# Four conditional transformer blocks on one core: queries and keys sent in two halves, and the filling work paced to the last step

## The chip, the cores and the metric

The kernel runs on one NeuronCore of a Trainium2 chip. The metric is the device time of one execution in microseconds. TensorE (PE) multiplies and transposes, VectorE (DVE) and ScalarE (ACT) work on its results in PSUM, GpSimd (POOL) adds, and SyncE (SP) issues nearly all DMAs from one queue, in order.

## The reference

The input `x` is 4 sequences of 512 tokens with 288 features, with one condition vector of 288 for each sequence. Four layers follow each other, all in float32.

```python
x = L0(x, cond)   # a conditional rotation: x + (z @ expm(A(cond)) - z) @ U.T, z = x @ U, U from a QR
x = L1(x, cond)   # attention with 16 heads of 18, then an MLP of 1152, both modulated and gated
x = L2(x, cond)   # the same, with a layer norm on each head's queries and keys
x = L3(x, cond)   # attention, then a mixture of 4 experts, 2 for each token
# in each attention:
qkv = modulate(layernorm(x)) @ w_qkv + b_qkv
attn = softmax(q @ k.T * 18 ** -0.5)
x = x + gate * ((attn @ v) @ w_proj + b_proj)
```

In the code the attention layers are counted 0, 1, 2 (reference layers 1, 2, 3). Layer 1 of the code is the one that normalizes queries and keys: each projected block needs the variance over the 18 features of a head.

## The kernel before

After the rotation the kernel goes through 12 items, n = 0 to 11: item n is sequence n % 4 in layer n // 4. `attend(n, ...)` does the attention of item n in 32 steps, 8 for each of 4 groups (G) of 4 heads. In every step PE computes one pair of score tiles `p_s` for the group that comes 10 steps later (`maxima`); DVE reduces the pair to its row maxima (`TENSOR_REDUCE store<-p_s`). In the same step PE computes one pair of transposed scores `p_st` (`weigh`), and ACT takes its exponential into `e`. In even steps `give_values` multiplies the weights of two earlier steps with the values (`p_av`). In step 6 of each group, steps 6, 14, 22 and 30 of an item, `take_maxima` transposes the maxima of the next group (`p_m`) and DVE subtracts them. `p_s` and `p_st` share two PSUM pairs, so `p_s` of a step needs the reduction of the step before to be over. A step is here the stretch from one `p_st` to the next.

Since the maxima run 10 steps ahead, step 22 of item n already reads queries and keys of item n + 1. All else is filling work, drawn from generators that yield a cost in microseconds. `attend` adds `total / 32` to a balance `left` in every step, and half a microsecond more in odd steps and less in even ones, and draws from `fill` until the balance is spent. The fill of item n is, in this order: the first part of `project(n + 1)`, up to where it yields `None`; `finish(n - 1)`, which multiplies the attention output of the item before with `w_proj` (`p_o`, four times) and adds it to `x`; the rest of `project(n + 1)`; and `layernorm(n - 1)`, the transposes `p_t` that feed the MLP. Small DVE steps (`normalize`, which makes `xn`, and `invert`, which multiplies `oc` by `rb`) come from a second list, one in each step. After the 32 steps, what is left of the fill is drawn at once, and `mlp(n - 1)` follows. After item 11 come the experts.

`project(n)` computes five blocks of queries and keys, `p_qk` 0 to 4 (126 rows each, the last 72), and four blocks of values, `p_v`. Each is two matmuls over 128 features (called `qk` and `v` below) and a tail over the last 32; the blocks go in pairs, so that the two tails run beside each other. A block is evicted into a `stage` tile and written to a DRAM scratch `qd` (L1076), from where eight DMAs bring the heads to their rows of `Q` and `K` (L1113) and four more clear a row (L1115). Queries are rows 0 to 287 of `qd`, keys 288 to 575. In layer 1 the eviction has three parts: ACT squares and DVE adds the bias; then PE sums the squares (`p_var`) and ACT makes the factor; then DVE scales (`SCALAR_TENSOR_TENSOR stage`) and POOL adds (L1075). The second part is drawn while the next pair is multiplied. In every item the third pair (`p_qk` 4, `p_v` 0) is finished at once, and then all is sent. Blocks `p_qk`, `p_v`, `p_var`, `p_o`, `p_m`, `p_t` share three PSUM banks (`pmm`).

The order of DMAs on SP's queue is made by the framework's scheduler, not by the text. The order on PE and DVE inside an attend follows the text.

Of the kernel before, what the change touches and what calls it, by code (L numbers as in the profile page):

```python
# [9 lines left out]
F32 = mybir.dt.float32  # L10
# [6 lines left out]
B, T, C = 4, 512, 288  # L17
# [4 lines left out]
H, HD, HS = 16, 18, 32  # L22
VS = HD + 1
NG = 4
HP = 7
QP = HP * HD
QK = 2 * C
NQ = -(-QK // QP)
# [19 lines left out]
def cond_seq_kernel(ctx: ExitStack, tc: tile.TileContext, a: dict, out: bass.AP):  # L48
# [18 lines left out]
    dma = nc.sync.dma_start  # L67
# [11 lines left out]
    def pmm(name):  # L79
        return ps.tile([128, 512], F32, tag="mm", name=name, bufs=3)  # L80
# [4 lines left out]
    def pacc(name):  # L85
        return ps.tile([128, 512], F32, tag="acc", name=name, bufs=1)
# [49 lines left out]
    def strip(i):  # L136
        return slice(i * TAIL, (i + 1) * TAIL)
# [89 lines left out]
    Q = [t[:, 0:NG * T].rearrange("p (g t) -> p g t", t=T) for t in store]  # L227
    K = [t[:, NG * T:2 * NG * T].rearrange("p (g t) -> p g t", t=T) for t in store]
# [7 lines left out]
    zero_row = rows.tile([4, NG * T], F32, name="zero_row")  # L236
# [432 lines left out]
    def layernorm(l, part, b, dst, norm):  # L669

        for _ in norm:
            pass
        for _ in to_featT(dst, b, XN.pop((l, part, b)), modT[l][:, 2 * part + 1], modT[l][:, 2 * part], 2 + part):
            yield 0.6
# [353 lines left out]
    with tc.tile_pool(name="attn", bufs=2) as at:  # L1028
# [15 lines left out]
        def project(n, norm):  # L1044

            l, b = divmod(n, B)
            wqk, wv = WA[l][:2]
            h = hT[0]
            yield from layernorm(l, 0, b, h, norm)
            qd = scratch.tile([2 * H, HD, T], F32, tag="qd", name=f"qd{n}")  # L1050
            flat = qd.rearrange("h d t -> (h d) t")

            def qk_job(m):
                w = min(QP, QK - m * QP)
                cols = slice(m * QP, m * QP + w)
                p = pmm(f"p_qk{n}_{m}")

                def evict():
                    bias = QB[l][0:w, m:m + 1]
                    t = at.tile([QP, T], F32, tag="stage", name=f"stage{n}_{m}", bufs=3)[0:w]  # L1060
                    if l != 1:
                        scalar.activation(t, p[0:w], AF.Identity, bias=bias, scale=scol[0:w, m:m + 1])
                    else:
                        tmp = at.tile([128, 2, T], F32, tag="e", name=f"tmp{n}_{m}", bufs=6)
                        sq, rs = tmp[0:w, 0, :], tmp[0:w, 1, :]
                        scalar.activation(sq, p[0:w], AF.Square, bias=bias)
                        vector.tensor_scalar(t, p[0:w], bias, None, ALU.add)
                        yield 0.0
                        pv = pmm(f"p_var{n}_{m}")
                        matmul(pv[0:w], varsel.rearrange("p h d -> p (h d)")[0:w, 0:w], sq, start=True, stop=True)  # L1070
                        scalar.activation(rs, pv[0:w], AF.Ln, bias=eps5[0:w])
                        scalar.activation(rs, rs, AF.Exp, scale=-0.5)
                        yield 0.86
                        vector.scalar_tensor_tensor(t, t, gains[0][0:w, m:m + 1], rs, ALU.mult, ALU.mult)
                        nc.gpsimd.tensor_scalar(t, t, gains[1][0:w, m:m + 1], None, ALU.add)  # L1075
                    dma(flat[cols], t)  # L1076
                return p[0:w], 0.86, lambda k, r: (wqk[r, k, cols], h[r, k, :]), evict

            def v_job(j):
                p = pmm(f"p_v{n}_{j}")  # L1080

                def evict():
                    (scalar.copy if j % 2 else vector.tensor_copy)(
                        V[n % 2][:, j, :, 0:HD], p[:, :C].rearrange("p (h d) -> p h d", d=HD))
                    yield from ()
                return p[:, :C], 0.49, lambda k, r: (h[r, k, j * 128:(j + 1) * 128], wv[r, k, :]), evict

            jobs = [(qk_job, m) for m in range(NQ)] + [(v_job, j) for j in range(NT)]
            later = []
            for i in range(0, len(jobs), 2):  # L1090
                pair = []
                for job, arg in jobs[i:i + 2]:
                    p, cost, operands, evict = job(arg)
                    for k in range(KW):
                        matmul(p, *operands(k, slice(0, 128)), start=(k == 0), stop=False)
                        yield cost
                    pair.append((p, operands, evict))
                for e in later:
                    yield from e
                for q, (p, operands, evict) in enumerate(pair):  # L1100
                    matmul(p, *operands(KW, strip(q)), start=False, stop=True)

                later = [e for e in [evict() for p, operands, evict in pair] if next(e, None) is not None]
                yield 0.95
                if i <= NQ - 1 < i + 2:
                    for e in later:
                        yield from e
                    later = []

                    src = qd.rearrange("(s g i) d t -> s i d g t", s=2, i=4)  # L1110
                    for s, t in enumerate((Q[n % 2], K[n % 2])):
                        for q in range(4):
                            dma(t[q * HS:q * HS + HD], src[s, q])  # L1113
                    for q in range(4):
                        dma(Q[n % 2][q * HS + HD:q * HS + VS], zero_row[q:q + 1].rearrange("a (g t) -> a g t", t=T))  # L1115
                    there.add(n)
                    yield None

        def maxima(G, step):

# [8 lines left out]
        def take_maxima(G):  # L1129

            n, g = divmod(G, NG)
            p = pmm(f"p_m{G}")
            for j in range(NT):
                transpose(p[:, j * 128:(j + 1) * 128], M[G % 2][:, j].rearrange("p h r -> p (h r)"), ident)
            vector.tensor_sub(Q[n % 2][:, g, :], Q[n % 2][:, g, :], p)
# [71 lines left out]
        def attend(n, fill, total, norms):  # L1207

            left = 0.0
            for step in range(8 * NG):  # L1210
                g, s = divmod(step, 8)
                G = NG * n + g
                ahead, mstep = divmod(8 * G + s + LOOK, 8)
                if ahead < NG * NB:
                    while ahead // NG not in there:
                        next(fill)
                    maxima(ahead, mstep)
                E.append(weigh(G, s))
                if s == 8 - 2 and G + 1 < NG * NB:
                    take_maxima(G + 1)  # L1220
                if s % 2 == 0:
                    give_values()
                left += total / (8 * NG) + (0.5 if s % 2 else -0.5)
                next(norms, None)
                while left > 0:
                    cost = next(fill, "end")
                    if cost == "end":
                        break
                    left -= cost or 0.0
                if s % 2:  # L1230
                    ready.append((G, s // 2))
            for _ in fill:
                pass
            for _ in norms:
                pass

        def give_values():

            if not ready:
                return  # L1240
            G, c = ready.pop()
            if c == 0:
                PO[0] = pacc(f"p_av{G}")
            sum_values(G, PO[0], c, E[:2])
            del E[:2]
            if c == NT - 1:
                t = at.tile([128, T], F32, tag="o", name=f"o{G}", bufs=3)
                scalar.copy(t, PO[0])
                n, g = divmod(G, NG)
                if g == 0:  # L1250
                    S[n] = (scratch.tile([H, T], F32, tag="sd", name=f"sd{n}"),
                            scratch.tile([H, HD, T], F32, tag="od", name=f"od{n}"))
                dma(S[n][0][4 * g:4 * g + 4, :], t.rearrange("(h r) c -> h r c", r=HS)[:, HD])
                for h in range(4):
                    dma(S[n][1][4 * g + h], t[h * HS:h * HS + HD])
# [29 lines left out]
        E, ready, PO, S, there, norms = [], [], [None], {}, set(), {}  # L1285
# [33 lines left out]
        for n in range(NB):  # L1319
            l, b = divmod(n, B)  # L1320
# [48 lines left out]
            if 2 <= n < 2 + 2 * NE:  # L1369
                fill_table(n - 2)  # L1370
            attend(n, itertools.chain(*fill), total, first_ready(side))
            if n == 2 or n == B + 2:
                projection_bias(l + 1)
# [183 lines left out]
```

## Time and profile before

| | us |
|---|---|
| median of 3 runs (2065.1 to 2071.37) | 2068.3 |
| the profiled execution, its own time | 2073.4 |
| its span, first to last instruction | 2071.7 |
| attends 1, 2, 7, 8, step 0 to step 31 | 91.2, 87.3, 87.2, 87.2 |
| attends 3, 4, 5, 6 (they project layer 1) | 92.9, 93.3, 103.7, 93.0 |
| attends 9, 10, 11 | 87.4, 97.8, 101.0 |

The page gives busy times over the whole span. What an attend does is read from the timeline, step by step: a step that is longer than its matmuls has idle time on PE, and the bracket behind the next `p_s` says how long and what ended it. The windows view gives the mean granted clock of PE for a stretch.

### The profile page before, as it was taken

What the parts mean: (1) busy time and instruction counts of PE and PEld (TensorE: products, weight loads), DVE (VectorE), ACT (ScalarE), POOL (GpSimd) and SP (SyncE); (2) the same over time, 40 slices, a digit from 0 to 9 for tenths busy, and PEclk for the clock granted to TensorE, in tenths of its full rate; (3) what the DMA queues carried; (4) which work ended last, traced back from release to release, by engine and by line L of the source; (5) the groups of instructions that cost most, each with busy time, mean ns of one, the idle gap of its engine ahead of it and who ended that gap; (6) DMA issues with size and microseconds to landing.
All of it is one profiled execution on the core that took longest, in us unless ns stands there. A gap on an engine that the chain in (4) does not pass through costs nothing. (4 is left out here: it accounts for less than half of the span.)

```text
span 2071.7 us, 26248 instructions
## 1 busy us (share of the span) xinstructions
PE 1887.7 (91%) x10269; PEld 935.6 (45%) x10269; DVE 928.4 (45%) x1953; ACT 783.6 (38%) x1169; POOL 251.9 (12%) x362
## 2 busy tenths in 40 slices
PE   6769879999999999899999999998987888999998
PEld 4544223343523434234234353333332266788886
DVE  6764646346164362552644626345576234211111
ACT  5122454444254343453544434434444222221221
POOL 1000010001010020010100000000000122233232
PEclk9578999999999999999999999999999689999999
DMA  3212152031131221511213112161212265576673
GB/s 97 71 40 62 36 147 84 22 89 36 25 85 30 70 62 42 136 42 54 72 26 77 42 54 81 21 134 35 83 46 66 86 222 167 182 242 200 211 241 97
DMA packets 89419, 187.23 MB, mean 90 GB/s; under 512 B 25453, under 2 KB 50456, under 8 KB 86802
## 3 DMA queue, kind: packets, MB, share of 16 engines
q1 hardware_dynamic: 77462, 103.39, 19.1%
q0 software_dynamic: 11248, 79.79, 11.9%
q10 hardware_dynamic: 584, 2.36, 0.3%
q8 instruction: 81, 1.33, 0.3%
q14 instruction: 44, 0.36, 0.1%
HBM read 152.49 MB, written 55.45 MB: 100 GB/s over the span
## 5 line engine op out<-in xcount | busy, mean ns | idle before, releaser
L60 ACT ACTIVATE e<-p_st 128x1024 f32<-128x1024 f32 x384 | 392.7, 1023 | 650.7 <-PE p_st L60 646.3
L60 DVE TENSOR_REDUCE store<-p_s 128x2 f32<-128x1024 f32 x384 | 470.3, 1225 | 364.5 <-PE p_st L60 320.7
L60 PE MATMUL p_s<-store 32*128 32x512 f32 x1536 | 442.2, 648 | 82.5 <-DVE store L60 81.3
L60 PE MATMUL p_st<-store 32*128 32x512 f32 x1536 | 445.7, 659 | 0.9 <-DVE store L60 0.9
L60 PEld LDWEIGHTS p_s<-store 32*128 32x128 f32 x1536 | 120.0, 185 | 315.3 <-DVE store L60 228.2
L60 PE MATMUL p_av<-e,store 128*32 128x512 f32 x1536 | 212.8, 627 | 2.2 <-ACT e L60 2.2
L60 PE MATMUL p_he<-hTe,store 128*128 128x256 f32 (+1 forms) x1026 | 188.4, 390 | 4.2 <-DVE hTe L60 4.2
L60 PE MATMUL p_ye<-store,hide 128*128 128x288 f32 x684 | 171.4, 409 | 0.0
L60 PEld LDWEIGHTS p_he<-hTe,store 128*128 128x128 f32 (+1 forms) x1026 | 151.4, 191 | 37.7 <-issue 13.6
L695 POOL TENSOR_TENSOR x<-x,gated 128x288 f32<-128x288 f32 x80 | 63.9, 799 | 841.6 <-DVE gated L60 841.6
L60 PE MATMUL p_qk<-hT,wqk 128*126 128x512 f32 (+1 forms) x360 | 163.1, 622 | 0.3 <-DVE store L60 0.3
L60 ACT ACTIVATE hide<-p_he,store 128x256 f32<-128x256 f32 x171 | 68.5, 478 | 245.1 <-PE p_he L60 244.3
L60 PE MATMUL p_h<-hT,w 128*128 128x512 f32 (+1 forms) x432 | 153.5, 610 | 5.2 <-DVE store L60 5.2
L60 PEld LDWEIGHTS p_ye<-store,hide 128*128 128x128 f32 x684 | 128.2, 190 | 36.7 <-ACT hide L60 2.3
L60 PE MATMUL p_y<-w,hid 128*128 128x288 f32 x576 | 141.8, 407 | 0.0
L60 DVE TENSOR_TENSOR gated<-p_y,gate 128x288 f32<-128x288 f32 x32 | 14.6, 457 | 283.0 <-PE p_y L60 283.0
L60 PEld LDWEIGHTS p_y<-w,hid 128*128 128x128 f32 x576 | 108.8, 190 | 35.5 <-issue 6.1
L60 PEld LDWEIGHTS p_st<-store 32*128 32x128 f32 x1536 | 118.2, 187 | 12.1 <-issue 9.1
L60 PEld LDWEIGHTS p_h<-hT,w 128*128 128x128 f32 (+1 forms) x432 | 62.1, 189 | 95.1 <-issue 84.9
L60 PE MATMUL p_o<-wp,oc 126*128 126x288 f32 (+1 forms) x288 | 99.4, 468 | 1.3 <-DVE oc L60 1.3
L60 PEld LDWEIGHTS p_qk<-hT,wqk 128*126 128x126 f32 (+1 forms) x360 | 47.1, 178 | 95.9 <-issue 94.3
L60 DVE COPY hTe<-p_te 128x512 f32<-128x512 f32 x19 | 13.1, 690 | 169.2 <-PE p_tf L60 117.8
(248 smaller groups left out, 1728.8 us busy)
## 6 DMA issues: line engine op xcount, KB each, us to landing
store<-qd SPq DMA_DIRECT2D x96, 144.0 KB
qd<-stage SPq DMA_DIRECT2D x48, 252.0 KB
od<-o SPq DMA_DIRECT2D x192, 36.0 KB
rd<-rd SPq DMA_DIRECT2D x12, 576.0 KB
oc<-od SPq DMA_DIRECT2D x24, 252.0 KB
rb<-rd SPq DMA_DIRECT2D x24, 252.0 KB
etab<-in_L_cond_w_dram SPq DMA_DIRECT2D x4, 1296.0 KB
etab<-in_L_cond_w_dram SPq DMA_DIRECT2D x8, 576.0 KB
```

Of the source, the lines that this page charges most:

```text
L60: ins = f(*args, **kw)
L695: nc.gpsimd.tensor_add(x[b][:, j, :], x[b][:, j, :], t)
```

## The change

The eight DMAs from `qd` become sixteen, in two halves of four each for queries and for keys: half 0 brings head groups 0 and 1, half 1 groups 2 and 3. Half 0 needs blocks 0 to 3 and is sent behind the second pair, half 1 behind the third. In layer 1 the third pair is no longer finished at once: its variance comes behind the main matmuls of the fourth pair, and each half is sent one pair later than in the other layers, half 1 and the `None` in the middle of the fourth pair (`p_v` 1 and 2). There are four `stage` buffers instead of three, and two `o` buffers instead of three. In steps 6, 14 and 22 of an item, and in 30 (where a next group exists), 0.6 is taken off the balance of the fill.

```diff
-                    t = at.tile([QP, T], F32, tag="stage", name=f"stage{n}_{m}", bufs=3)[0:w]
+                    t = at.tile([QP, T], F32, tag="stage", name=f"stage{n}_{m}", bufs=4)[0:w]
...
+            def send(half):
+
+                src = qd.rearrange("(s g i) d t -> s i d g t", s=2, i=4)
+                gs = slice(half * NG // 2, (half + 1) * NG // 2)
+                for s, t in enumerate((Q[n % 2], K[n % 2])):
+                    for q in range(4):
+                        dma(t[q * HS:q * HS + HD, gs], src[s, q, :, gs])
+                for q in range(0 if half else 4):
+                    dma(Q[n % 2][q * HS + HD:q * HS + VS], zero_row[q:q + 1].rearrange("a (g t) -> a g t", t=T))
+                there.add(n)
+
+
+            parts = {(-(-(C + C // 2) // QP) - 1) // 2 * 2: 0, (NQ - 1) // 2 * 2: 1}
...
                 for e in later:
                     yield from e
+                if l == 1 and i - 2 in parts:
+                    send(parts[i - 2])
+                    if parts[i - 2]:
+                        yield None
                 for q, (p, operands, evict) in enumerate(pair):
                     matmul(p, *operands(KW, strip(q)), start=False, stop=True)
 
                 later = [e for e in [evict() for p, operands, evict in pair] if next(e, None) is not None]
                 yield 0.95
-                if i <= NQ - 1 < i + 2:
-                    for e in later:
-                        yield from e
-                    later = []
-
-                    src = qd.rearrange("(s g i) d t -> s i d g t", s=2, i=4)
-                    for s, t in enumerate((Q[n % 2], K[n % 2])):
-                        for q in range(4):
-                            dma(t[q * HS:q * HS + HD], src[s, q])
-                    for q in range(4):
-                        dma(Q[n % 2][q * HS + HD:q * HS + VS], zero_row[q:q + 1].rearrange("a (g t) -> a g t", t=T))
-                    there.add(n)
-                    yield None
+                if l != 1 and i in parts:
+                    send(parts[i])
+                    if parts[i]:
+                        yield None
...
                 if s == 8 - 2 and G + 1 < NG * NB:
                     take_maxima(G + 1)
+                    left -= 0.6
...
-                t = at.tile([128, T], F32, tag="o", name=f"o{G}", bufs=3)
+                t = at.tile([128, T], F32, tag="o", name=f"o{G}", bufs=2)
```

The order of PE's instructions in the two built programs shows how the fill moves. Steps that are not listed keep theirs. Attends 1, 7, 8 are as 2, attends 4 to 6 as 3. In the table `qk` and `v` are one matmul of a block, `tail` the one over the last 32 features, `var` a `p_var`, `o0` to `o3` the four `p_o`, `t0` to `t2` groups of four transposes, `m` the `p_m`. Every even step has `p_av` besides. Lengths are those of the trace before, in us.

| step | attend 2 before | us | after | attend 3 before | us | after | attend 9 before | us | after |
|---|---|---|---|---|---|---|---|---|---|
| 6 | m | 3.4 | m | m | 2.7 | m | m, 2 tails | 3.6 | m |
| 7 | 2 qk | 3.0 | qk | 2 qk | 3.0 | qk | qk | 2.6 | 2 tails, qk |
| 8 | | 2.5 | qk | qk | 3.1 | qk | qk | 3.1 | |
| 9 | 2 qk | 3.0 | qk | var0, var1 | 4.0 | qk, var0 | qk | 2.5 | 2 qk |
| 10 | | 2.5 | qk | | 2.5 | | qk | 3.1 | |
| 11 | 2 tails, qk | 2.9 | 2 tails | 2 tails, qk | 2.9 | var1, 2 tails | 2 tails | 2.5 | qk, 2 tails |
| 12 | | 2.5 | qk | qk | 3.2 | qk | qk | 3.1 | |
| 13 | qk, v | 2.6 | qk | 2 v | 2.5 | qk, v | qk | 2.5 | qk |
| 14 | m, v | 3.3 | m | m, var2 | 4.1 | m | m, v | 3.3 | m |
| 15 | 2 tails, o0 | 3.8 | 2 v, 2 tails | var3, 2 tails | 2.5 | v, var2 | v, 2 tails | 2.5 | qk, v |
| 16 | | 2.5 | | | 4.1 | var3 | | 2.6 | v |
| 17 | o1 | 2.9 | o0 | var4, o0 | 3.7 | 2 tails, v | o0 | 2.9 | 2 tails |
| 18 | | 2.5 | | | 2.5 | v | o1 | 3.9 | o0 |
| 19 | o2 | 2.9 | o1 | o1 | 2.9 | 2 v, var4 | | 2.5 | o1 |
| 20 | o3 | 3.9 | o2 | o2 | 3.9 | | o2 | 3.9 | |
| 21 | | 2.6 | o3 | o3 | 2.9 | o0, o1 | o3 | 2.9 | o2 |
| 22 | m, v | 3.3 | m | m | 2.7 | m | m | 2.7 | m |
| 23 | 3 v | 2.7 | | 2 v | 2.5 | o2 | v | 2.5 | o3 |
| 24 | 2 tails | 2.6 | v | v | 2.7 | | v | 2.7 | |
| 25 | 2 v | 2.3 | 3 v | v, 2 tails, v | 3.1 | o3 | 2 v, 2 tails | 2.5 | v |
| 26 | tail | 2.5 | 2 tails | v | 2.8 | | | 2.7 | v |
| 27 | t0, t1 | 3.5 | 2 v | tail, t0 | 3.4 | 2 tails, v | 2 v | 2.5 | 2 v, 2 tails |
| 28 | | 2.5 | tail | t1 | 2.7 | v | tail | 2.5 | |
| 29 | t2 | 2.5 | t0, t1 | t2 | 2.5 | tail, t0 | | 2.4 | 2 v |
| 30 | m | 3.1 | m | m | 3.1 | m | m | 2.7 | m |
| 31 | MLP | | t2, MLP | MLP | | t1, t2, MLP | | 2.5 | tail |

On DVE the last `xn` of attend 2 stands in step 27 before and in step 28 after. In attend 3 all four stand in step 29 after (one each in steps 25 and 26 and two in 27 before). In attends 0, 10 and 11 the fill moves by one to two steps in the same way.

## The prediction

> **What bounds the kernel now.** I read the page first, then the timeline inside the attends, then their windows.
>
> ```profile
> span 2071.7 us, 26248 instructions
> PE 1887.7 (91%) x10269; PEld 935.6 (45%) x10269; DVE 928.4 (45%) x1953; ACT 783.6 (38%) x1169; POOL 251.9 (12%) x362
> ...
> L60 DVE TENSOR_REDUCE store<-p_s 128x2 f32<-128x1024 f32 x384 | 470.3, 1225 | 364.5 <-PE p_st L60 320.7
> L60 PE MATMUL p_s<-store 32*128 32x512 f32 x1536 | 442.2, 648 | 82.5 <-DVE store L60 81.3
> ```
>
> TensorE (PE) is busy in 91% of the span; of its 184 us of idle, 82.5 stand ahead of `p_s`, nearly all ended by VectorE (DVE) work. The loop is on the timeline of attend 2:
>
> ```profile
> 484.08 0.70 PE L60 MATMUL p_s<-store 32*128 32x512 f32 x2 [0.32 <-DVE store L60]
> ...
> 485.15 1.92 PE L60 MATMUL p_o<-wp,oc 126*128 126x288 f32 x6
> 485.26 1.23 DVE L60 TENSOR_REDUCE store<-p_s 128x2 f32<-128x1024 f32 x1 [0.65 <-PE p_st L60]
> 487.00 0.70 PE L60 MATMUL p_s<-store 32*128 32x512 f32 x2
> ...
> 490.92 0.70 PE L60 MATMUL p_s<-store 32*128 32x512 f32 x2
> ...
> 492.09 1.23 DVE L60 TENSOR_REDUCE store<-p_s 128x2 f32<-128x1024 f32 x1 [0.61 <-PE p_st L60]
> 493.37 0.77 PE L60 MATMUL p_s<-store 32*128 32x512 f32 x2 [1.32 <-DVE store L60]
> ```
>
> A step without filling work lasts 490.92 to 493.37, 2.45 us: `p_s` runs 1.17, its reduction 1.23, and only then is the PSUM pair free. That is the floor. PE itself needs 1.07 for `p_s` and `p_st` (484.08 to 485.15), and in even steps 1.07 more for `p_av`. So an odd step hides about 1.4 us of fill, an even one 0.3; fill beyond that lengthens the step, room left empty is lost. The step with `p_o` (484.08 to 487.00) lasts 2.9.
>
> In the attends that project layer 1 the DVE queue sets some steps:
>
> ```profile
> 612.18 0.75 DVE L60 SCALAR_TENSOR_TENSOR stage<-stage,qn_g,tmp 126x512 f32<-126x512 f32 x1 [0.58 <-ACT tmp L60]
> ...
> 612.85 0.74 DVE L60 TENSOR_SCALAR stage<-p_qk,qkb 72x512 f32<-72x512 f32 x1
> 613.51 0.44 DVE L60 COPY store<-p_v 128x288 f32<-128x288 f32 x1
> 613.87 1.21 DVE L60 TENSOR_REDUCE store<-p_s 128x2 f32<-128x1024 f32 x1
> 615.14 0.19 PEld L60 LDWEIGHTS p_s<-store 32*128 32x128 f32 x2 [2.46 <-DVE store L60]
> ```
>
> Evictions stand ahead of the reduction, and PE waits. Two attends are longer for another reason, by their windows (length, busy time of PE, PEld, DVE, ACT, POOL, then granted clock):
>
> ```profile
> 431.10:518.40 87.30, 80.76 (x489) 28.43 (x490) 53.92 (x78) 44.56 (x54) 6.00 (x11) 1.00 0.27 74
> 563.50:656.40 92.90, 86.57 (x499) 29.37 (x500) 60.39 (x88) 50.40 (x64) 11.73 (x10) 1.00 0.32 66
> 828.70:932.50 103.80, 94.20 (x501) 31.49 (x502) 60.76 (x88) 50.46 (x64) 11.71 (x10) 0.92 0.36 89
> ...
> 1612.00:1650.00 38.00, 36.82 (x100) 11.87 (x104) 5.83 (x19) 9.12 (x12) 6.27 (x7) 0.55 0.31 114
> ```
>
> Attend 5 holds the same work as attend 3 and takes 10.9 us more, at a clock of 0.92; the end of attend 11 ran at 0.55.
>
> **The change, part by part.** I go by the table of steps above: each new step gets the length of a measured step with the same content, or else 1.07 plus its fill.
>
> *Pacing, attends 1, 2, 7, 8.* The 0.6 taken off in steps 6, 14, 22, 30 moves fill later. Steps 7 to 12: two `qk` in one odd step (3.0) and an empty even step (2.5) become one each (2.5 and 3.1 from attend 3's step 8), so 16.4 becomes 16.8; a small loss, since an even step has no room. Steps 13 to 16: 2.6, 3.3, 3.8, 2.5 become 2.5, 2.7, 2.95, 2.5, since `o0` leaves step 15: 12.2 to 10.65. Steps 17 to 22: 2.9, 2.5, 2.9, 3.9, 2.6, 3.3 become 2.9, 2.5, 2.9, 3.9, 2.9, 2.7; step 21 had 1.3 of idle and now holds `o3`: 18.1 to 17.8. Steps 23 to 28: 2.7, 2.6, 2.3, 2.5, 3.5, 2.5 become 2.5, 2.7, 2.7, 2.6, 2.4, 2.5: 16.1 to 15.4. There step 27 waited 1.1 for the last `xn`, issued in that very step; after, `xn` ends in step 28 and the transposes come in 29, which stays at 2.6 (it was 2.5) and holds two transposes instead of one. Step 30 stays at 3.1. Sum 68.4 to 66.35. `t2` (0.6) goes into step 31 ahead of the MLP, where PE waits 0.9 for a reduction now (attends 1, 7, 8): covered there, 0.6 in attend 2. Gain 2.1 each, 8.4 in four.
>
> *Attends 9 and 10.* In attend 9 the even steps 8, 10, 12 held a `qk` and lasted 3.1; emptied, they last 2.5, and the odd steps 7, 9, 11 that take these go from 2.6, 2.5, 2.5 to 3.0. With the rest of its columns steps 6 to 31 go from 73.2 to 70.9: 2.3. Steps 14 to 31 of attend 10 go from 53.5 to some 51; there many small DVE operations of the routing move too, so I take 2.0. Attends 0 and 11 keep their work and their empty steps: 0.
>
> *Layer 1, attends 3, 4, 6.* For: step 9 (4.0, two variances, the second waiting 0.8 for ScalarE) becomes 3.2; step 14 loses `var2` (4.1 to 2.7); step 16 loses its 1.5 of idle but takes `var3` (4.1 to 3.2); step 17 loses `var4` and `o0` (3.7 to 2.5). Against: step 11 now queues `oc` and four stage operations on DVE, 0.66 apart, behind its reduction (2.4) and ahead of the next, which so ends at 2.4 + 3.3 + 1.25 = 6.95; step 11 lasts 2.85 and step 12 the other 4.1, not 3.2. In step 21 two `p_o` meet, and the pair `v1`, `v2` holds two of the three PSUM banks until step 27, so the second, 1.9 long, starts only behind the first one's `gated` at about 3.6: 2.9 to 5.5. In step 29 the first transpose drains the normalization: reduction to 2.4, four `xn` of 0.36 each, the last transpose 0.3: 2.5 to 4.2. Steps 7 to 30 sum to 73.3 before and 72.7 after, and 0.4 of `t1`, `t2` sticks out ahead of the MLP. Gain 0.2 each, 0.6 in three; the bounds are -2 (the three new waits half as long again) and +3 (none of them).
>
> *Fourth buffer, attend 5.* The only wait for a stage buffer that I find is there:
>
> ```profile
> 868.91 0.75 DVE L60 TENSOR_SCALAR stage<-p_qk,qkb 126x512 f32<-126x512 f32 x1 [1.17 <-POOL stage L1075]
> ...
> 870.85 0.29 PEld L60 LDWEIGHTS p_s<-store 32*128 32x128 f32 x2 [4.62 <-DVE store L60]
> ```
>
> The buffer takes the 1.17 away, but the `oc` before it still waits for `rb` until 865.73, and one more stage operation (0.66) stands in the queue: 0.5. I leave the half clock of attend 5 where it is.
>
> *Sending in halves.* 8 more DMAs per projection, about 0.35 us of SP each (four `store<-qd` issue in 1.65), 2.8 per attend on a queue that waits most of the time. Queued behind a send's wait for `qd` are the `o` stores of the group and later `oc<-od`. In attend 2 the last send was issued at 479.1, the DMA share is zero from 485, and the first reader is at 493.37; in attend 3 it is 624.6, 629 and 631.1. In layer 1 the second half now ends about 10 us after step 21 begins, but its first reader is the third head group, 16 steps after step 22. Cost 0; if this cover were gone, up to 5 us in each of the four. Two `o` buffers instead of three: a buffer returns after 16 steps, over 40 us, while its five DMAs issue within 10 us of the copy, even in attend 5: 0.
>
> Sum: 8.4 + 2.3 + 2.0 + 0.6 + 0.5, about 14 us. The profiled execution took 2073.4 us, 1.7 around its span and 5.1 above the median; 2073.4 - 14 is 2059.4, and from the median 2068.3 it is 2054.
>
> **Rivals.** *The steps only trade (same).* The floor stays and no work is removed; if the new steps queue on DVE as attend 3 does now, the four plain attends give 0.5 each, layer 1 loses 2 each, the rest 2: some 4 lost, 4 won, 2062 to 2070. For: steps 7 to 12 lose by my own table. Against: the idle of steps 21 and 27 is plainly in the trace. That the fourth buffer has nothing to remove outside attend 5 belongs here.
>
> *The clock is granted again (much faster).* Attend 5 lost 10.9 us, and from 1612.06 to 1646.82 seven `p_st`, four `p_av`, four `p_o` and one `p_m` took 34.8 us, where their full-speed spacings (1.05, 1.0, 1.84, 0.6) make 19.3. If moved steps miss one or both, 10 to 26 us more: 2028 to 2044. For: attend 4 has a longer idle (1.9) in step 16 than attend 5 (1.6) and stayed at 1.00. Against: what precedes both stretches, the late `rb` and the sparse steps of attend 11, is unchanged, and the three times lie within 0.3%. [...]
>
> *Layer 1 falls to half clock (slower).* After the change attends 3, 4, 6 have new idles: 1.0 in step 12, 1.5 in step 29. Attend 5 shows the price, 10.9 each. It decides from two of three: 2054 + 22 is 2076, with all 2087. For: the second low stretch of attend 5 began after an idle of 1.6. Against: idles of 1.5 to 1.9 in attends 3, 4, 6 did not do it, and neither did 1.1 to 1.3 in the others.
>
> **How the numbers follow.** Forecast (gain 7 to 20) 0.58, clock granted 0.15, trade 0.18, half clock 0.09. A measurement of this kernel tells about 0.3%, 6.2 us, from no change. So faster 0.73, same 0.18, slower 0.09. The range reaches into one clock stretch won (2035) and to the trade (2068).
>
> **What would show it.** Right: attends 1, 2, 7, 8 near 85 us, step 21 filled, no wait for `xn` ahead of the transposes; attends 3, 4, 6 within 2 us of before, step 21 near 5.5, step 29 near 4.2; no `p_s` ended by a DMA. Wrong: plain attends unchanged, `p_s` waiting for `store<-qd`, DVE waiting for POOL's `stage`, or a clock below 1.00 in other attends than 5, 10 and 11.

## The result, and the profile after

| | before | after |
|---|---|---|
| median of 20 runs each, us | 2067.2 (2060.0 to 2081.1) | 2060.0 (2040.7 to 2063.2) |
| the profiled execution, us | 2073.4 | 2047.1 |
| its span, us | 2071.7 | 2045.4 |
| attends 1, 2, 7, 8, step 0 to 31 | 91.2, 87.3, 87.2, 87.2 | 87.7, 84.5, 84.5, 84.5 |
| attends 3, 4, 5, 6 | 92.9, 93.3, 103.7, 93.0 | 91.8, 90.2, 99.5, 90.2 |
| attends 9, 10, 11 | 87.4, 97.8, 101.0 | 84.5, 100.0, 86.6 |

The changed kernel is faster: the ratio is 0.9933, interval 0.9911 to 0.9955, which is 13.9 us of 2067.2. The difference of the medians, 7.2, is smaller because the changed kernel's twenty times lie in two bands, 8 at 2040.7 to 2047.1 and 12 at 2058.6 to 2063.2, and nothing between; the ratio goes over all of them. Their mean granted clocks part as well, 0.956 to 0.959 and 0.945 to 0.948. What parts the bands is the subject of the last experiments. The profiled execution is of the lower one.

From the page of the changed kernel, first its span and busy times, then the two groups of the step:

```profile
span 2045.4 us, 26383 instructions
PE 1876.4 (92%) x10269; PEld 933.1 (46%) x10269; DVE 929.2 (45%) x1953; ACT 784.1 (38%) x1169; POOL 255.5 (12%) x362
...
L60 DVE TENSOR_REDUCE store<-p_s 128x2 f32<-128x1024 f32 x384 | 470.4, 1225 | 360.4 <-PE p_st L60 324.5
L60 PE MATMUL p_s<-store 32*128 32x512 f32 x1536 | 445.5, 653 | 75.5 <-DVE store L60 74.4
```

The work is the same, 10269 matmuls; the idle ahead of `p_s` went from 82.5 to 75.5. On the timeline of attend 2 step 21 begins with the `p_s` at 489.37 and ends with the next:

```profile
489.37 0.70 PE L60 MATMUL p_s<-store 32*128 32x512 f32 x2
...
490.44 1.92 PE L60 MATMUL p_o<-wp,oc 126*128 126x288 f32 x6
492.28 0.70 PE L60 MATMUL p_s<-store 32*128 32x512 f32 x2
```

It now holds `o3` and no idle stands ahead of the next `p_s`; before, this step waited 1.32. In layer 1 the three places that the prediction named are on the timeline of attend 4: DVE's queue of step 11, the second `p_o` of step 21, the first transposes of step 29.

```profile
725.87 0.68 DVE L60 TENSOR_TENSOR oc<-oc,rb 126x512 f32<-126x512 f32 x1
726.47 1.45 DVE L60 SCALAR_TENSOR_TENSOR stage<-stage,qn_g,tmp 126x512 f32<-126x512 f32 x2
727.84 1.40 DVE L60 TENSOR_SCALAR stage<-p_qk,qkb 126x512 f32<-126x512 f32 x2
729.16 1.21 DVE L60 TENSOR_REDUCE store<-p_s 128x2 f32<-128x1024 f32 x1
...
755.82 1.92 PE L60 MATMUL p_o<-wp,oc 126*128 126x288 f32 x6 [0.55 <-DVE gated L60]
...
779.06 1.35 PE L60 MATMUL p_t<-ident,xn 128*128 128x128 f32 x4 [1.17 <-DVE xn L60]
```

The five operations ahead of the reduction (`oc`, two scalings, two additions of the bias) run without a gap, and none waits for a stage buffer. In attend 5 the buffer wait is gone too, but its place is taken by a longer wait for `rb` (DVE, then PE, then SP's queue of DMAs):

```profile
861.57 0.69 DVE L60 TENSOR_TENSOR oc<-oc,rb 126x512 f32<-126x512 f32 x1 [5.46 <-DMA rb<-rd]
...
866.09 1.22 PE L60 MATMUL p_s<-store 32*128 32x512 f32 x2 [6.27 <-DVE store L60]
...
842.57 0.81 SPq L1176 DMA_DIRECT2D rd<-sums  x1
854.58 0.55 SPq L1178 DMA_DIRECT2D rd<-rd  x1
...
858.41 1.18 SPq L1181 DMA_DIRECT2D rb<-rd  x3
```

The windows of attends 2, 4 and 5 and of the end of attend 11 (length, busy times, granted clock, DMA share, GB/s):

```profile
430.80:515.40 84.60, 79.71 (x487) 27.66 (x486) 53.87 (x78) 42.41 (x51) 6.08 (x11) 1.00 0.27 76
...
692.80:783.00 90.20, 84.93 (x490) 28.54 (x489) 59.98 (x88) 47.17 (x60) 12.47 (x11) 1.00 0.25 72
822.90:922.40 99.50, 88.71 (x489) 29.54 (x488) 60.37 (x88) 47.28 (x60) 12.10 (x10) 0.95 0.38 92
...
1582.00:1620.00 38.00, 34.27 (x208) 11.30 (x204) 17.72 (x50) 16.33 (x18) 6.29 (x7) 0.97 0.33 119
```

The last line stands against 0.55 before: in this execution the long half clock at the end of attend 11 is absent.

From start to start the 26.3 us of the two profiled executions divide so: 16.3 are won by the start of attend 11, 14.4 in attend 11 (the clock), and 4.4 are lost among the experts. From the last step to the end the profiled executions below take 420 to 426 us with the same expert code (427.3 and 430.6 in the two where a long half clock runs on into this part), in no order that follows their edits (425.4 here and 420.3 in a kernel below that differs only in layer 1), so I put the 4.4 down to this execution; no run shows its cause. That the 14.4 are the clock's is borne out further down: with extra matmuls that keep the long half clock away, attend 11 takes 84.4 in the kernel before and 84.3 in the changed one.

### The profile page after: what moved, and what is told of

Same layout as the page of the kernel before. It is cut to its first block, busy times and chain, and to the rows that moved or that the text cites. A ratio compares the mean times of both kernels' runs of the same rounds, so it can differ in the third digit from the quotient of the medians.

```text
span 2045.4 us, 26383 instructions
## 1 busy us (share of the span) xinstructions
PE 1876.4 (92%) x10269; PEld 933.1 (46%) x10269; DVE 929.2 (45%) x1953; ACT 784.1 (38%) x1169; POOL 255.5 (12%) x362
## 5 line engine op out<-in xcount | busy, mean ns | idle before, releaser
L60 PE MATMUL p_s<-store 32*128 32x512 f32 x1536 | 445.5, 653 | 75.5 <-DVE store L60 74.4
L60 PE MATMUL p_qk<-hT,wqk 128*126 128x512 f32 (+1 forms) x360 | 167.6, 630 | 0.3 <-DVE store L60 0.3
L60 PE MATMUL p_o<-wp,oc 126*128 126x288 f32 (+1 forms) x288 | 92.6, 442 | 3.5 <-DVE gated L60 2.2
L1515 POOL DMA_INDIRECT out_dram<-ye,idx x38 | 62.6, 1648 | 216.7 <-DVE ye L60 138.0
```

The source lines that it names most:

```text
L60: ins = f(*args, **kw)
L1515: tc.keep_in_program_order(nc.gpsimd.indirect_dma_start(out_rows if t >= EARLY else out_rows[0:2 * T], bass.IndirectOffsetOnAxis(ap=idx[:, ...
```

## The experiments

### What each part is worth in layer 1

Six kernels take the change apart. In all of them with the 0.6 the attends 1, 2, 7 and 8 take 84.5 to 87.8 us, as in the changed kernel; they differ in layer 1.

**The pacing alone.** The kernel before, with this line:

```diff
                     take_maxima(G + 1)
+                    left -= 0.6
```

> The kernel before with only the 0.6 taken off the balance in steps 6, 14, 22 and 30; whole sends, third pair finished at once, three stage and three o buffers. Theory of pacing (moving the fill out of even steps and into steps that had idle time is the whole gain): attends 1, 2, 7, 8 take 84.5 to 87.7 us and attend 9 84.5, as in the changed kernel; in layer 1 the fill of steps 7 to 16 is the same as in the changed kernel, so attends 3, 4, 6 take about 90 to 91; attend 11 begins 12 to 16 us earlier than before. Theory of the late variances (in layer 1 the later third pair brings the gain): attends 1, 2, 7, 8, 9 as above, attends 3, 4, 6 stay near 93, and attend 11 begins 8 to 10 earlier. Total by the first 2053 to 2056, or 15 to 18 less where the end of attend 11 is spared its half clock.

Measured: ratio 1.0054 (1.0017 to 1.0092), slower. The plain attends are as expected (attend 2 84.5, 7 and 8 84.6 and 84.5). Attends 3, 4, 6 take 98.3, 97.2, 97.2, worse than before, which neither theory had, and attend 11 begins 6.5 later than before instead of 8 to 16 earlier. The timeline of attend 4 shows why (DVE, POOL, PE):

```profile
732.59 0.74 DVE L60 TENSOR_SCALAR stage<-p_qk,qkb 126x512 f32<-126x512 f32 x1
736.70 0.75 DVE L60 TENSOR_SCALAR stage<-p_qk,qkb 126x512 f32<-126x512 f32 x1 [3.36 <-DMA qd<-stage]
...
732.12 3.51 POOL L1075 TENSOR_SCALAR stage<-stage,qn_b 126x512 f32<-126x512 f32 x2 [33.05 <-DVE stage L60]
...
738.63 1.22 PE L60 MATMUL p_s<-store 32*128 32x512 f32 x2 [4.22 <-DVE store L60]
```

The pacing brings the scaling of blocks 0 and 1 and the biasing of blocks 2 and 3 into the same step. Block 3 is the fourth owner of three stage buffers: DVE waits until POOL has added to block 0 and its store to `qd` is over, and the reduction, and with it `p_s`, waits behind DVE. The granted clock of attend 4 is 0.96. The twelve times lie in two groups, 2064.3 to 2072.4 and 2084.2 to 2092.6; the profile is of the upper one and has 54.6 us at half clock from the end of attend 11 on.

**The change without the pacing.**

```diff
                     take_maxima(G + 1)
-                    left -= 0.6
```

> The changed kernel without the 0.6: halves, late variances, four stage buffers and two o buffers stay. Theory of pacing: attends 1, 2, 7, 8, 9 as in the kernel before (91.2, 87.3, 87.2, 87.2, 87.4), attends 3, 4, 6 near 93, total within 4 us of the kernel before. Theory of the late variances: attends 3, 4, 6 near 90.5, total some 7 less than before.

Measured: ratio 1.0098 (1.0064 to 1.0131). The plain attends are back at 87.2 to 91.6, as expected of the pacing. Attends 3, 4, 6 take 96.7, 96.7, 95.2, again worse than before, against both theories: without the 0.6 the last variance and `o0` meet in step 19 (4.8) and `o2` falls into step 22 (4.9). In attends 3 and 4 a half clock of 3.4 us in step 28 comes on top.

**Three stage buffers.** The changed kernel with `bufs=3` for `stage`.

> The changed kernel with three stage buffers instead of four; all else of the change stays. Buffer theory (with the fill paced, four scaled or biased blocks stand in stage at once in step 11 of layer 1, so with three DVE waits for POOL's add and the store of the oldest; the fourth buffer is what makes the pacing pay in layer 1): step 12 of attends 3, 4 and 6 takes 7 to 8 with 4 of idle, as in the run with the pacing alone, and half clock comes with it; these attends take 96 to 98 instead of 90 to 92, attend 5 some 4 more than 99.5; total 2062 to 2066 or, with the half clock at the end of attend 11, 2080 to 2090. Rival (the prediction's own term: the buffer is waited for in attend 5 alone): attends 3, 4, 6 stay at 90 to 92, total within 3 of the changed kernel.

Measured: ratio 0.9993 (0.9958 to 1.0028). Step 12 of attends 3, 4 and 6 takes 7.9 with 4.2 of idle, against 4.4 and 0.8 with four buffers, DVE waits 3.34 for `qd<-stage`, and half clock (736.8 to 743.6 in attend 4) follows; the attends take 96.7, 96.6, 96.9. The buffer theory holds; the fourth buffer decides on 6 us in each of three attends, half clock included. Attend 5 takes 101.6, 2 more than in the changed kernel where 4 were expected.

**Pacing and buffer without the rest.** The kernel before with the 0.6, four `stage` and two `o` buffers.

> The kernel before with the 0.6 and the fourth stage buffer (and two o buffers, which give it its room); whole sends, third pair finished at once. Buffer theory: attends 3, 4, 6 take 89 to 91.5, attend 11 begins 14 to 18 earlier than before, and the total is the changed kernel's, 2042 or 2060. Theory of the late variances: attends 3, 4, 6 still need the later third pair and take 93 or more, attend 11 begins 6 to 10 earlier, total 2050 to 2068.

Measured: ratio 0.9922 (0.9888 to 0.9956), times in two bands. Attends 3, 4, 6 take 92.4, 92.7, 92.6: between the two theories. Step 12 is 4.4, so the buffer does its part; what is left shows at the boundary of steps 21 and 22:

```profile
753.00 1.92 PE L60 MATMUL p_o<-wp,oc 126*128 126x288 f32 x6
755.12 1.81 PE L60 MATMUL p_s<-store 32*128 32x512 f32 x3 [0.19 <-DMA store<-qd]
```

`p_s` waits for the rows of the heads, and its row of three lasts 1.81 ahead of the half clock that then follows for 3.4 us (757.5 to 760.9); step 21 takes 4.3, and 2.9 in the run below where only half of the rows has to come.

**Whole sends in the changed kernel.** The eight DMAs bring all groups at once, where the second half was sent.

```diff
-                gs = slice(half * NG // 2, (half + 1) * NG // 2)
+                if not half:
+                    return
...
-                        dma(t[q * HS:q * HS + HD, gs], src[s, q, :, gs])
-                for q in range(0 if half else 4):
+                        dma(t[q * HS:q * HS + HD], src[s, q])
+                for q in range(4):
```

> The changed kernel with the eight whole sends, issued where it sends the second half; all else stays. If the halves are worth nothing, as predicted: every attend within 0.3 of the changed kernel's but for the clock. Rival: in layer 1 step 22 reads the first head group soon after the later send, so a whole send comes too late there: p_s waits for store<-qd in step 22 of attends 3 to 6, by 1 to 5 us each, total 4 to 20 more.

Measured: ratio 1.0048 (1.0015 to 1.0081). The rival holds: attends 3, 4, 6 take 100.4, 100.2, 99.9, and `p_s` of step 22 in attend 4 waits for the rows:

```profile
769.00 2.29 PE L60 MATMUL p_s<-store 32*128 32x512 f32 x3 [4.70 <-DMA store<-qd]
```

Step 21 takes 11.3 instead of 5.4, part of it at half clock (765.5 to 775.7). The plain attends do not mind: 84.5 to 85.3. The times, 2070.0 to 2078.5 and 2092.4 to 2095.6, are some 30 above the changed kernel's bands, more than the 4 to 20 expected: attends 3, 4 and 6 take 8.6 to 10.0 longer than in the changed kernel, and in attend 4 the half clock, 10.2 us long, adds to the wait.

**The third pair finished at once.** The changed kernel, but with the last variances of layer 1 and the second half's send where the kernel before has them.

```diff
+                if l == 1 and parts.get(i):
+                    for e in later:
+                        yield from e
+                    later = []
+                    send(1)
+                    yield None
```

> The changed kernel with the third pair of layer 1 finished at once, as in the kernel before, and the second half sent there; the first half, the 0.6 and the buffers stay. If the later third pair is what brings attends 3, 4, 6 from the 92.5 of the run with pacing and fourth buffer alone to the changed kernel's 90.7, they are back at 92.5, with step 17 at 4.0 (1.0 of idle ahead of the waiting variance) and step 20 at 3.9, and the halves by themselves are worth nothing. If the halves bring it, the attends stay at 90.7. Total 2043 or 2062 by the first, 2042 or 2060 by the second.

Measured: 2034.6 median of 4 runs, ratio 0.9893 (0.9846 to 0.9940). Steps 17 and 20 are 4.0 and 3.9 as expected, but the attends are at 89.6, 89.7, 89.5, better than either theory: step 21 is 2.9 and step 29 3.4. So the halves bring the attends from 92.6 to 89.6, and the later third pair costs 0.5 to 2.2 an attend. Three of the four times are 2033.9 to 2034.9, below the lower band of the changed kernel.

Mean length of attends 3, 4 and 6, by parts, each row from one profiled execution with its half clock included:

| pacing | 4th buffer | halves | late third pair | us |
|---|---|---|---|---|
| | | | | 93.1 |
| x | | | | 97.6 |
| x | | x | x | 96.7 |
| x | x | | | 92.6 |
| x | x | | x | 100.2 |
| | x | x | x | 96.2 |
| x | x | x | x | 90.7 |
| x | x | x | | 89.6 |

No part has a price of its own here. Pacing alone costs 4.5; pacing and buffer together win 0.5 (the buffer without the pacing was not run); the late third pair costs 7.6 without the halves and 1.1 with them.

### The stall of attend 5

The changed kernel with the loads for layer 2 issued behind attend 5:

```diff
-            if n == 1 or n == B + 1:
+            if n == 1:
...
             attend(n, itertools.chain(*fill), total, first_ready(side))
...
+            if n == B + 1:
+                WA.append(load_attn(2, "L3_cond_w_qkv", "L3_cond_b_qkv", "L3_cond_w_proj", "L3_cond_b_proj"))
```

> The changed kernel with the ten loads of the attention weights of layer 2 issued behind attend 5 instead of ahead of it. Theory of the queue (the big loads at the start of attend 5 delay the sums and the reciprocal rows, so rb comes late and DVE waits 5.5 for it in step 12): step 12 of attend 5 falls from 9.9 to about 4.4, its half clock goes, attend 5 takes 90 to 92 instead of 99.5, total some 8 less. Rival (rb is late in attend 5 for another reason, or the loads now delay something in the MLP or in attend 6): attend 5 stays near 99, or as much is lost behind it.

Measured: ratio 0.9896 (0.9857 to 0.9936); bands at 2032.6 to 2040.6 and 2052.8 to 2057.2, each 6 to 8 below the changed kernel's. That the loads make `rb` late holds: `rd<-rd` is issued 4.9 behind `rd<-sums` instead of 12.0, DVE's wait for `rb` is gone, step 12 takes 4.4, and the window of attend 5 is that of attend 4 (first the two issues on SP's queue):

```profile
839.92 0.33 SPq L1176 DMA_DIRECT2D rd<-sums  x1
844.80 0.57 SPq L1178 DMA_DIRECT2D rd<-rd  x1
...
823.00:913.20 90.20, 84.92 (x492) 28.53 (x491) 60.01 (x88) 47.17 (x60) 12.15 (x10) 1.00 0.41 102
```

The place in SP's queue is only part of it. From the start of the attend `rd<-sums` is issued 2.7 earlier; the other 7.1 are the shorter way from it to `rd<-rd`, while the DMA share in 838 to 843 and 843 to 848 is 0.39 and 0.32 instead of 1.03 and 1.26. Whether the queue or the transfers of the loads hold this link was not separated.

### The clock at the end of attend 11

**Seven extra matmuls in the changed kernel.**

```diff
+        def warm(name):
+            p = pmm(f"p_w{name}")
+            matmul(p, ident, x[0].rearrange("p j c -> p (j c)")[:, 0:512], start=True, stop=True)
...
                 next(norms, None)
+                if n == NB - 1 and s % 2 and 8 < step < 22:
+                    warm(f"{n}_{step}")
```

> The changed kernel with one extra matmul of 128x512 (about 0.86 us) in each odd step 9 to 21 of attend 11, where PE otherwise idles 0.8 to 1.3; nothing reads its result. Clock theory (the two bands of times, near 2042 and near 2061, differ by a long half-clock stretch in steps 22 to 31 of attend 11, which idle time in the sparse steps ahead of it calls forth): without these idles the stretch does not come, every run falls near 2042 (2038 to 2047), the median about 17 below the changed kernel's. Rival (the stretch comes from something else, whatever PE does ahead of it): both bands stay, at 2042 and 2061 or a little above.

Measured: 2043.6 (2041.9 to 2047.8) in 5 runs, ratio 0.9882 (0.9844 to 0.9920): all in the lower band, 16.4 below the changed kernel's median. The idle of steps 9, 15, 19 and 21 was 1.0 to 1.3 and is 0.1 to 0.3; step 17, which holds transposes of its own, gets 0.7 longer.

**The same in the kernel before.**

> The kernel before with the same extra matmuls in attend 11. Clock theory: the stretch at 1612 to 1647 goes, attend 11 takes about 86 instead of 101, and nearly every run is about 15 faster, 2050 to 2055. Rival: attend 11 stays near 101 and the median within 3 of before.

Measured: 2059.0 (2052.4 to 2068.2) in 12 runs, ratio 0.9949 (0.9919 to 0.9978). In the profile attend 11 takes 84.4 instead of 101.0 at a clock of 0.98, as the clock theory has it; over the runs the gain is 11 (5 to 17), less than the 15 expected: only 4 of 12 lie in the 2050 to 2055 forecast for nearly all, and 5 are above 2060. Attend 5, which at 100.2 still has its stall, may be one cause of the spread; no run shows it.

The two kernels with the seven matmuls, measured side by side, compare before and after without the long half clock: 2059.0 and 2043.6, a difference of 15.4. So the change is worth about its 14 us with this stretch out of both.

**One extra matmul, in step 21.**

```diff
+                if n == NB - 1 and step == 21:
+                    warm(f"{n}_{step}")
```

> The changed kernel with one extra matmul only, in step 21 of attend 11, the last idle ahead of the steps that ran at half clock. If the idle just ahead decides on the long stretch: nearly all runs fall near 2042, as with the seven matmuls. If all the idle of steps 9 to 21 together decides: both bands stay, 2042 and 2060, in some such share as 8 to 12 of 20.

Measured: 9 of 12 runs at 2038.9 to 2047.4 and 3 at 2060.3 to 2064.0: both bands remain, so the idle just ahead does not decide alone. Whether this matmul helps at all is left open by 3 of 12 against 12 of 20. The profiled execution is of the upper band and shows what it is made of. Attend 11 and its end, in windows:

```profile
1531.20:1630.30 99.10, 85.88 (x454) 28.63 (x454) 48.96 (x103) 36.72 (x41) 9.26 (x11) 0.80 0.23 78
1597.00:1630.00 33.00, 33.00 (x82) 10.48 (x80) 4.40 (x12) 7.82 (x9) 6.28 (x7) 0.51 0.35 131
```

PE is busy in all of the 33 us and runs at 0.51; the trace has the half clock from 1597.5 to 1652.1. On its timeline the idle just ahead of it is no longer than 0.48:

```profile
1594.10 1.13 PE L60 MATMUL p_st<-store 32*128 32x512 f32 x4
...
1596.10 1.13 PE L60 MATMUL p_st<-store 32*128 32x512 f32 x4 [0.48 <-DVE places L60]
1597.15 1.69 PE L60 MATMUL p_av<-e,store 128*32 128x512 f32 x8
1598.77 2.08 PE L60 MATMUL p_st<-store 32*128 32x512 f32 x4
```

**Both cures together.** The changed kernel with the seven matmuls and the loads behind attend 5.

> The changed kernel with the loads of layer 2 behind attend 5 and the seven extra matmuls in attend 11. If the two act at different places and add up: all runs at 2032 to 2037, one band, attend 5 at 90 and attend 11 at 84 to 87, about 33 below the kernel before. If the clock only moves its stretch elsewhere: two bands again, 2034 and 2052, or a half-clock stretch of more than 10 in another place.

Measured: 2032.6 (2029.1 to 2035.6) in 5 runs, ratio 0.9852 (0.9830 to 0.9874), the fastest of the study; one band, as expected of two causes that add. The windows of attends 5 and 11:

```profile
822.10:912.40 90.30, 85.03 (x493) 28.65 (x492) 60.04 (x88) 47.13 (x60) 12.13 (x10) 1.00 0.40 102
1524.10:1606.80 82.70, 73.26 (x468) 25.69 (x468) 48.83 (x103) 36.48 (x41) 9.28 (x11) 1.00 0.28 94
```

**Extra matmuls in attends 0 and 10 too.** The condition becomes `step in {0: (15, 23, 29, 31), NB - 2: range(19, 32, 2), NB - 1: range(9, 22, 2)}.get(n, ())`.

> The same with extra matmuls also in attend 10 (odd steps 19 to 31) and in attend 0 (steps 15, 23, 29, 31), which hold idle of 1.3 to 2.5 and three to four stretches of half clock of 3.4 to 7 each. Clock theory: those stretches go, attend 10 from 100 to 94 to 97 and attend 0 and its end 2 to 4 shorter, total 2025 to 2031. Rival (steps without enough idle pay 0.9 for each, and the clock falls there anyway): 2034 to 2042.

Measured: 2035.5 (2032.3 to 2040.1) in 6 runs, ratio 0.9864 (0.9843 to 0.9885). The rival holds for attend 10: it takes 101.7 instead of 98.4, at the same clock of 0.95. Steps 23 and 25 had no room (5.2 and 3.4 instead of 4.2 and 2.5); another 1.6 are a half clock in step 11, which has no extra matmul, and step 30 gives 1.2 back. Attend 0 falls from 86.0 to 84.0, but attend 1 loses 5.1: it begins earlier, and DVE waits for the weights of the next layer.

```profile
309.25 1.35 DVE L189 TENSOR_REDUCE wmean<-wqk 128x64 f32<-128x1152 f32 x1 [3.73 <-DMA wqk<-in_L_cond_w_qkv_dram]
```

`p_s` waits 4.67 behind it, where it waited 1.79 in the run before this one, and a half clock of 6.8 us begins in this wait.

The later third pair undone, together with both cures, was not run.

## Why the prediction was right or wrong

By start-to-start differences of the profiled executions, in us:

| term of the sum | predicted | measured |
|---|---|---|
| attends 1, 2, 7, 8 | -8.4 | -9.7 |
| attend 9 | -2.3 | -2.8 |
| attends 3, 4, 6 | -0.6 | -5.0 |
| attend 5 | -0.5 | -3.8 |
| attend 10 | -2.0 | +2.2 |
| attend 0 and what lies ahead | 0 | +2.8 |
| sum to the start of attend 11 | -13.8 | -16.3 |

**The sum** of 14 stands beside 13.9 from the ratio, and so close a match is luck: layer 1 and attend 5 won 7.7 more than forecast, attend 10 and what lies ahead of attend 1 lost 7.0 that were not forecast, and the ratio is a mean over two bands, about 6 and 24 below the kernel before. The 15.4 with the long half clock out of both kernels says that the size is right all the same. The median, 2060.0, is higher than the 2054 forecast, since the upper band holds 12 of 20 runs.

**Pacing, plain attends: right, in mechanism and size.** Step 21 is filled, the transposes of step 29 no longer wait for `xn`, and the pacing alone gives 84.5. Step 30, which the prediction left at 3.1, became 2.7; `t2` ahead of the MLP was not covered in attends 1, 7 and 8, where step 31 went from 39.5 to 39.9. Attend 1 won 3.1, and 0.9 of it is not the pacing's: in its first steps DVE waits for the weights `wqk`, 2.43 before and 0.61 after.

**Layer 1: the step that failed.** Steps 11, 12, 21 and 29 came out at 2.5, 4.4, 5.4 and 4.1 where 2.85, 4.1, 5.5 and 4.2 were forecast, so the three new waits were read well. But steps 7 to 30 sum to 70.5 in attend 4, not 72.7: 1.9 of the difference lie in the other steps, 0.4 of it in step 30 again. The prediction does not list these steps; its own rule, with the lengths of its table and of the steps that it names, gives about 71.6 by my estimate, so some 1.0 seems to be a slip of addition. Start to start, attends 4 and 6 won 2.6 and 1.7 instead of 0.2; attend 3 won 0.7 and lost the rest to 3.4 us of half clock in step 30. So two signs named under "Right" and "Wrong" went against it: attends 4 and 6 moved by more than 2 us (3.1 and 2.8 from step 0 to 31), and attend 3 ran in part below full clock.

**The fourth buffer: right place for the wait before, wrong worth.** "The only wait for a stage buffer that I find is there" was read from the order of before. In the new order the same three buffers cost 6 in each of attends 3, 4 and 6 (96.7 against 90.7). The sum was not hurt, because it was made on the order with the buffer in.

**The halves: their cost was right, their worth was missed.** 8 more DMAs cost nothing that the runs show. But the prediction left out what whole sends would do in the new order: 92.6 instead of 89.6 with the third pair at its old place, 100.2 instead of 90.7 at the new one, where the wait of 4.70 is what it named as the price of a lost cover, up to 5 us. The 2 us of cover that it counted in attend 3 (629 to 631.1) were used up by the pacing: with whole sends and pacing `p_s` waits for `store<-qd`. The two `o` buffers cost nothing, as forecast: in the changed kernel no copy into `o` waits for a store, and the only idle ahead of the 48 copies, 2.6 us, is ended by `p_av`.

**The late third pair** had no term of its own. It costs 1.1 an attend in layer 1.

**Attend 5.** The prediction left the half clock "where it is"; with it, it left the largest single loss unexplained. The wait for `rb` grew from 2.3 to 5.5 and the idle of step 12 from 3.8 to 6.3, and still the attend got shorter, as 10.2 us of it ran at half clock instead of 17.1. The cause of the wait is the layer 2 loads issued ahead of it.

**Attend 10: wrong sign.** Steps 14 to 21 fell from 26.5 to 21.9, more than the gain forecast. Step 11 gave back 1.7 without any idle in it, and steps 22 to 31 gave back 5.2; the trace has 13.7 us of half clock in the attend instead of 6.8 (3.4 of it in step 11), and half of the routing's `p_logit` moved from step 21 to step 23 (4.2 instead of 2.5). Attend 0, which was to stay as it is, takes 1.5 more, with a half clock of 6.8 us instead of 3.4 at its end; the other 1.3 lie ahead of it, in code that did not change.

**The rivals.** The clock, granted again in 8 of 20 runs, was given 0.15: the prediction took a difference between executions of one program for one of the kernels, since three times of before lay within 0.3%. What ends such a stretch no run shows: PE was busy in all of the 33.0 us at 0.51 above. Trading did not happen. Half clock in attends 3, 4 and 6 did not come in the changed kernel beyond 3.4 us in attend 3 (648.8 to 652.2), but it came in kernels close to it: in attend 4, 6.8 us of it began in an idle of 4.2 (three buffers), and 10.2 us in a wait of 4.70 (whole sends).

## What to carry to other kernels

A wait that is absent from the trace of before is no proof that a buffer or an early transfer is worth nothing: make the new order first, then count how many owners a buffer set has in the fullest step, and when the first reader now comes. When several edits are made together, read them as a table of combinations; here the same late third pair costs 1.1 or 7.6, and the same pacing wins or loses. Where an engine has idle steps ahead of a stretch that matters, and the runs fall in two bands, cheap filling matmuls in those steps may be worth nearly as much as the edit under study (here 10 to 11 us by the ratios, against 13.9).

## What the runs showed of the hardware

In the traces of the kernel before and of the changed kernel the granted clock is either 1.0 or 0.5. 17 stretches at 0.5 end inside the trace before and 20 inside that of the changed kernel. The shortest, 10 and 12 of them, last 3.41 us, the others 6.83, 10.24, 30.72, 34.13 and 51.20, all whole multiples of 3.413; so are the distances between any two changes of the clock in the same trace. The 51.2 and the 30.7 lie ahead of the first attend in both (50.7 to 101.9 and 136.1 to 166.8 before), the 34.1 at the end of attend 11 before (1614.1 to 1648.2, with PE busy in all of it).

The same program runs with and without the long stretch. With one extra matmul the profiled execution has 54.6 us of it, with PE busy in all of the 33.0 shown above, and a mean granted clock of 0.948; the nine faster executions have 0.956 to 0.960. Over the changed kernel and the variants with three buffers, with pacing and buffer alone, with whole sends, with the third pair at once and with the loads moved, 31 of 69 runs are in the upper band; with the seven matmuls, none of 16. So matmuls in those steps keep the stretch away in the changed kernel; whether it is the idle time that they fill, which of it counts, and what ends the stretch, stays open.

Where the changes of the clock lie goes along with it. Counted on from any of them in steps of 3.413 us, the next point after the start of step 22 of attend 11 comes 1.99 us later in the profile before (1612.06 to 1614.05) and 1.08 in the changed kernel's (1596.60 to 1597.68). It is 2.0 to 2.8 in the four profiles that have a stretch of 17.1 us or more there (before, pacing alone, no pacing, one extra matmul), and 0.9 to 1.1 in the six that, also without the seven matmuls, have none. The kernel before with the seven matmuls has none either, at 2.5. These are single executions of different programs, so it is not shown that the place of these points decides.
